# Graph kernel of four layers: the beginning of layer 3 in another order (alternate chunks per tile, reads ahead of casts, parts spread over nine steps), and the last layernorm in three tiles

## The chip, the cores and the metric

The kernel runs on one core of one Trainium2 chip. The metric is the device time of one execution in microseconds (us); less is better. Five engines work side by side, each through its own queue in order: TensorE (PE, matmuls; its weight loads are shown as PEld), VectorE (DVE), ScalarE (ACT), GpSimd (POOL) and SyncE (SP, which here only issues transfers).

## The reference

3327 nodes with 64 features, and a dense weighted adjacency `adj`. Four layers, each followed by a residual and a layernorm:

```python
x = _layernorm(x + _L0_gnn_ref(t, x, adj))       # 1 - 0.1 x - 0.01 sum(x * (adj @ x)), constant per node
x = _layernorm(x + _L1_gnn_ref(x, adj, att_W, att_b))   # hyperbolic attention over all pairs
x = _layernorm(x + _L2_gnn_ref(x, adj, W))
x = _layernorm(x + _L3_gnn_ref(x, adj, weight, bias))
# layer 2, two hops
for k in range(2):
    agg = adj @ x
    x = jnp.tanh(jnp.concatenate([agg, x], axis=1) @ W[k])
# layer 3: each node takes its last 100 neighbours, the last with weight 1, each before with half of the next
support = x @ weight
mask = (adj != 0); rank = jnp.cumsum(mask, axis=1); deg = rank[:, -1:]
k = jnp.minimum(deg, 100.0); pos = rank - (deg - k)
w = mask * jnp.where(pos > 0, 0.5 ** (k - pos), 0.0)
out = w @ support + bias
```

## The kernel before

Nodes are padded to 26 blocks of 128 (`NB`), in two halves of 13; `adj` is held transposed in HBM, and a block is 128 rows of it by 3328 columns, 1.7 MB. The last four blocks stay in SBUF for the whole run (`kept`), two more for layer 2; the others are streamed by SP's queue into a few slots, and a slot's next transfer waits until PE has read the slot. The instructions of PE, ACT and DVE stand in the order in which the code writes them (`manual_schedule`); each engine takes its queue in order, and an instruction that must wait holds all behind it on its engine. [...]

**End of layer 1** (`near_end`). A serial chain of small operations on 128x26 numbers goes back and forth between DVE and ACT (one tanh, two square roots). PE has nothing to do but a few idle matmuls (`awake`). At the end DVE writes x2 in five groups (L1441), the last operand of each in a PSUM tile `pm`.

**Layer 2** (`layers`, first part). x2 is transposed (`turned`, L339), multiplied with the upper half of W (`top`, L349, into `lj`), and then for each block eight matmuls (`add`, L395) add to four chunks of 416 columns in both halves, in the four banks of two PSUM tiles `cnt`: chunks 0 and 1 in the first tile, 2 and 3 in the second. `bottom` (L386) adds x times the lower half of W. Two hops; `chunk_end` adds the last two or three kept blocks for one chunk and takes the tanh on ACT (L471). In the second hop the order of blocks is: six that are still in SBUF from the first hop, then the kept ones with five streamed blocks behind each. Between, `pw_3` (L436) multiplies layer 3's weight with the centring matrix, and ACT copies it back (L437).

**Layer 3.** For every step q (half h, block jb from the last to the first, 52 steps in all) DVE makes a mask (L331, three steps ahead), PE counts with two triangular matrices (`count` and `advance`, L491) into `cnt[0]` and `cnt[1]`, whose bits read as int16 are the bf16 powers of two (`read`: ACT L506 or DVE L504), and PE multiplies these weights `w` with the node values (`products`, L689, and every three steps a group of twelve for the lowest part, L704). Reading `cnt[c]` and advancing it exclude each other. In the loop, ACT reads chunk 0 and DVE chunk 1. The node values are split in three bf16 parts (`first_part`, `rest_of`, `other_parts`: ACT, DVE, then ACT and POOL).

**The beginning of layer 3** is written out by hand and overlaps the end of hop 2. The blocks come in four parts A, B, C, E. For each: `finish` (PE, L558, tile `both`, two buffers), `squares` (ACT), `sums` and `roots` (DVE, nine short operations), `factor` and `x3_of` or `hid_out`, then the split. The first steps' reads and advances stand between. With the loop's first steps (q from `LEAD`, which is 3) stand the splits of C and E, three operations in one step each:

```python
with_step = {
    LEAD: lambda: (first_part(C), rest_of(C), other_parts(C)),
    LEAD + 1: lambda: (first_part(E), rest_of(E), other_parts(E)),
    LEAD + 2: lambda: x3_later(C),
    LEAD + 3: lambda: x3_later(E),
}
```

**Half ends.** After a half's 26 steps, `sums_out` moves the sums to SBUF (ACT and DVE, a chunk each), `sum_of_parts` turns them back to rows by node in 13 matmuls of two passes (L729, one PSUM tile `pr_o`), and a layernorm follows: `half_out` for the first half, a piece with each step of the second, and `last_out` for the second half, in three groups of nodes (6, 4, 3).

Of the kernel before, what the change touches and what calls it, by code (L numbers as in the profile page):

```python
# [10 lines left out]
F32 = mybir.dt.float32  # L11
# [62 lines left out]
def kernel(  # L74
# [220 lines left out]
    def layer_3_constants():  # L295
# [2 lines left out]

        nc.gpsimd.tensor_scalar(w3_dg, w3_dg, float(2**27), None, ALU.mult)


    @with_exitstack
    def layers(ctx, x2, x3, kept, ready, ahead_ctx, strm):
# [41 lines left out]
        def node_products(ps, hT, w, g, n, name):  # L345
# [11 lines left out]
        x2T = x3.rearrange("p n d -> p (n d)")  # L357
        hT = x2T
        l3c = ctx.enter_context(
            tc.tile_pool(name="l3c", bufs=1, space=PSUM, reuse_waits="tile")  # L360
        )

        cnt = [l3c.tile([P, 2, 512], F32, name=f"cnt_{c}")[:, :, :CW] for c in range(2)]
        acc = [cnt[c // 2][:, c % 2, :] for c in range(CPH)]
        pinned = ctx.enter_context(ExitStack())
        pinned.enter_context(
            tc.manual_schedule(engines={mybir.EngineType.DVE, mybir.EngineType.Activation})
# [1 line left out]
        with tc.tile_pool(name="l2p", bufs=2, space=PSUM, reuse_waits="tile") as l2p:  # L369
            for k in range(2):  # L370
# [39 lines left out]
                others = [jb for jb in range(NB) if jb not in kept and jb not in ready]  # L410
                share = -(-len(others) // len(stay))
                order = list(ready)
                for i, jb in enumerate(stay):
                    order += [jb] + others[i * share : (i + 1) * share]
                blocks = {**ready, **kept}

                if k == 0:
                    turned(0)
                    turned(1)
                    top(0, nc.scalar.copy)  # L420
                    turned(2)
# [12 lines left out]

                    pw = l2p.tile([P, 4 * P], F32, tag="pt", name="pw_3")[:, :P]
                    nc.tensor.matmul(pw, center, w3_dg, start=True, stop=True)  # L436
                    nc.scalar.copy(w3_dg, pw)  # L437

                    warm_t = small.tile([P, 1], F32, tag="warm", name="warm_t")
                    nc.scalar.activation(warm_t, ones, AF.Tanh)  # L440
                    order = order[2:]
                else:
                    top(0)
                    bottom(0)
                    bottom(1)
# [153 lines left out]
        def x3_of(i):  # L599
            scaled(i, both[i][0], x3)  # L600
# [19 lines left out]
        with tc.tile_pool(name="l3t", bufs=2, space=PSUM, reuse_waits="tile") as l3t:  # L620
            chunk_end(3)
            with_x2(3)
            chunk_end(2)
            with_x2(2)
            finish(l3t, A)
            squares(A)
            chunk_end(1)
            sums(A)
            roots(slots(A))
            factor(A)  # L630
            with_x2(1)
            finish(l3t, B)
            squares(B)
            x3_of(A)
            sums(B)
            first_part(A)
            count(1, tri, 0, True)
            read(1, 0, False)
            rest_of(A)
            chunk_end(0)  # L640
            roots(slots(B))
            with_x2(0)
            other_parts(A)
            finish(l3t, C)
            count(0, tri, 0, True)
            advance(1, 0)
            squares(C)
            read(0, 0, False)
            factor(B)
            x3_of(B)  # L650
            first_part(B)
            sums(C)
            finish(l3t, E)
            hid_out(C)
            advance(0, 0)
            rest_of(B)
            read(1, 1, True)
            squares(E)
            hid_out(E)
            advance(1, 1)  # L660
            read(0, 1, False)
            other_parts(B)
            sums(E)
            advance(0, 1)
            roots(slice(0, 2 * sum(parts[C])))
            read(1, 2, False)
            advance(1, 2)
            read(0, 2, False)
            advance(0, 2)
            factor(C)  # L670
            factor(E)

        l3a = ctx.enter_context(
            tc.tile_pool(name="l3a", bufs=2, space=PSUM, reuse_waits="tile")
# [45 lines left out]
            nc.vector.tensor_scalar(to[1], acc[h, 1], b3_sb, None, ALU.add)  # L720
            return accT

        def sum_of_parts(h, accT):

            pr = acc_tile(f"pr_o_{h}").rearrange("p e k -> p (e k)")[:, : NBH * D]
            pr = pr.rearrange("p (n d) -> p n d", d=D)
            xh, hh, sh = (by_half(t)[:, :, h] for t in (x3, hid, sq))
            for b in range(NBH):
                nc.tensor.matmul(  # L729
                    pr[:, b, :], accT[:, b * P : (b + 1) * P], center2, start=True, stop=True  # L730
                )
            return pr, xh, hh, sh
# [10 lines left out]
        def last_out(h, accT):  # L743

            pr, xh, hh, sh = sum_of_parts(h, accT)
            v = small.tile([P, NBH], F32, tag="v_out", name=f"v_out_{h}")
            parts = (slice(0, 6), slice(6, 10), slice(10, NBH))

            def added(s):
                nc.vector.tensor_tensor(hh[:, s], pr[:, s], xh[:, s], ALU.add)  # L750
                nc.scalar.activation(sh[:, s], hh[:, s], AF.Square)

            def summed(s):
                nc.vector.tensor_reduce(v[:, s], sh[:, s], axis=AX.X, op=ALU.add)

            added(parts[0])
            added(parts[1])
            summed(parts[0])
            added(parts[2])
            summed(parts[1])  # L760
            summed(parts[2])
            r = rsqrt_of(v, NBH)

            rows = N - h * HALF - (NBH - 1) * P
            for s, queue in zip(parts, (nc.sync, nc.scalar, nc.sync)):
                nc.vector.tensor_tensor(
                    hh[:, s], hh[:, s], spread(r[:, s], s.stop - s.start), ALU.mult
                )
                if store(queue, h, hh, s):
                    nc.scalar.dma_start(out[N - rows :], hh[:rows, NBH - 1])  # L770

        def half_out(h, accT):

            pr, xh, hh, sh = sum_of_parts(h, accT)
            v = small.tile([P, NBH], F32, tag="v_out", name=f"v_out_{h}")
            parts = (slice(0, 8), slice(8, NBH))
            yield
# [9 lines left out]
            for s in parts:  # L787
# [3 lines left out]
                store(nc.sync, h, hh, s)  # L791
                yield

        first_out = None
        with_step = {
            LEAD: lambda: (first_part(C), rest_of(C), other_parts(C)),
            LEAD + 1: lambda: (first_part(E), rest_of(E), other_parts(E)),
            LEAD + 2: lambda: x3_later(C),
            LEAD + 3: lambda: x3_later(E),
        }  # L800
        for q in range(LEAD, len(steps) + LEAD + 1):
            read(0, q, False)
            read(1, q, True)
            if q == NB + LEAD:
                accT = sums_out(0)
            masks(q + AHEAD)
            with_step.pop(q, lambda: None)()
            p = q - LEAD if q < NB + LEAD else q - LEAD - 1
            for c in range(2):
                if q < len(steps):  # L810
                    advance(c, q)
                if q != NB + LEAD:
                    products(p, c)
            if q == NB + LEAD:
                first_out = half_out(0, accT)
            if first_out is not None:
                next(first_out, None)
        last_out(1, sums_out(1))

# [14 lines left out]
    with tc.tile_pool(name="l1", bufs=1) as l1:  # L834
# [426 lines left out]
        def near_end(mT, xm, sq_e, t_e, x2):  # L1261
# [3 lines left out]
            with tc.tile_pool(name="l1e", bufs=1) as l1e, tc.tile_pool(  # L1265
# [395 lines left out]
        with norms.Else():  # L1661
            with ExitStack() as arm:
                x1 = xc
                with tc.tile_pool(name="g1m", bufs=1) as g1m:
                    m = g1m.tile([P, NB, D + 1], F32, name="m")
                    any_norm(m, x1)
                    layer_3_constants()
                    blocks = blocks_ahead(arm)
                    any_end(m, x1, x2)
                layers(x2, xc, *blocks)  # L1670
# [31 lines left out]
```

## Time and profile before

| | us |
|---|---|
| median of 3 runs | 576.31 (576.22 to 577.29) |
| the profiled execution | 575.76 |
| its span, first to last instruction | 573.9 |
| layer 1, attention (until the last pq) | about 222 |
| end of layer 1, to the first transposed x2 | 222 to 244 |
| layer 2, hop 1 and hop 2 | 244 to 330, 330 to 414 |
| layer 3, both halves | 404 to 559 |
| last layernorm and store | 559 to 574 |

The page gives busy time by engine; the waits say who waited for whom on an engine; the stretches give busy time of each engine within a window; the timeline shows single instructions with their start. Times are from one profiled execution. The mean granted PE clock is 0.985 of full speed.

### The profile page before, as it was taken

Reading aid. Unit: us, or ns where it says so; the run is one execution under the profiler, and the core shown is the slowest. Engines: PE = TensorE matmul, PEld = TensorE weight load, DVE = VectorE, ACT = ScalarE, POOL = GpSimd, SP = SyncE. Lnnn points to the kernel's source line nnn. Section 1 sums busy time; section 2 is a strip of 40 time slices with the busy share of each in tenths; the row PEclk is TensorE's granted clock in tenths of the full one; section 3 lists DMA queues with packets and bytes.
Section 4 is the critical chain, followed back from the end, with each engine's and each line's share of the span. In section 5 each row is a group of like instructions: output and inputs, shape, how many; then the busy total and the mean of one; then the engine's idle time right before and its main releaser. Section 6 shows DMA issues by size and latency. Waiting matters only on the chain.

```text
span 573.9 us, 7452 instructions
## 1 busy us (share of the span) xinstructions
PE 529.7 (92%) x2827; PEld 223.3 (39%) x2827; DVE 364.6 (64%) x528; ACT 276.7 (48%) x329; POOL 216.9 (38%) x134
## 2 busy tenths in 40 slices
PE   8899989999999999689999999998989999999992
PEld 5522222222222224254444354433444555555542
DVE  6899999999999998920000010400388777797724
ACT  4899999998999997321000100000263333343321
POOL 3799999999999998100000000000020000000000
PEclk9899999999999999989999999999999999999996
DMA  8976765750767653999999029998608996699701
GB/s 290 358 270 211 225 216 206 233 184 1 230 208 221 233 181 120 399 428 404 421 429 408 10 99 422 370 423 351 239 13 296 322 334 230 208 282 366 246 2 35
DMA packets 34037, 145.27 MB, mean 253 GB/s; under 512 B 10285, under 2 KB 11975, under 8 KB 28871
## 3 DMA queue, kind: packets, MB, share of 16 engines
q1 hardware_dynamic: 31655, 144.11, 69.0%
q10 hardware_dynamic: 2336, 0.59, 0.5%
q8 instruction: 24, 0.39, 0.3%
q14 instruction: 22, 0.18, 0.1%
HBM read 143.23 MB, written 0.87 MB: 251 GB/s over the span
## 4 chain that ended last, share of the span: by engine, by line
PE 63%; DVE 19%; ACT 8%; DMA 4%; issue 4%; POOL 0%; DVEq 0%; POOLq 0%
PE cnt L395 22%; PE pq L1028 12%; DVE v L1049 12%; PE cnt L491 11%; PE acc L689 6%; DMA at_l<-in_adjT 4%; ACT sg L1004 3%; PE acc L704 3%; ACT pq L1041 2%; DVE a L1040 2%; PE pn_l L349 1%; PE both L558 1%; PE pr_o L729 1%; PE cnt L386 1%; PE idle L864 1%
## 5 line engine op out<-in xcount | busy, mean ns | idle before, releaser
L1015 POOL TENSOR_TENSOR u<-sg,at 128x832 f32<-128x832 f32 x88 | 169.9, 1958 | 3.1 <-ACT sg L1004 2.7
L1028 PE MATMUL pq<-riT,ljT 64*128 64x416 f32 x416 | 100.2, 560 | 15.2 <-DVE v L1049 6.3
L1040 DVE SCALAR_TENSOR_TENSOR a<-pq,dl,u 128x832 f32<-128x832 f32 x104 | 112.0, 1077 | 3.0 <-PE pq L1028 2.9
L1041 ACT ACTIVATE pq<-pq,al,gas 128x832 f32<-128x832 f32 x104 | 104.9, 1010 | 15.2 <-DVE a L1040 14.2
L1049 DVE SCALAR_TENSOR_TENSOR v<-pq,a 128x832 f32<-128x832 f32 x104 | 105.6, 1016 | 1.1 <-ACT pq L1041 0.7
L1061 PE MATMUL acc<-v,xv 128*64 128x416 f32 x416 | 95.4, 537 | 0.1
L395 PE MATMUL cnt<-at_l,lj 128*64 128x416 f32 x480 | 86.5, 513 | 2.1 <-DMA at_l<-in_adjT 2.1
L1004 ACT ACTIVATE sg<-lb,rb 128x1664 f32<-128x1664 f32 (+1 forms) x53 | 87.3, 1647 | 0.1
L506 ACT ACTIVATE w<-cnt 128x832 int16<-128x832 f32 x54 | 46.5, 864 | 72.3 <-PE cnt L491 72.3
L471 ACT ACTIVATE hT<-cnt 128x416 f32<-128x416 f32 x8 | 4.1, 517 | 146.0 <-PE cnt L395 146.0
L618 POOL TENSOR_TENSOR s<-sq,s 128x384 bf16<-128x384 f32 (+1 forms) x4 | 4.1, 1025 | 185.9 <-ACT s L617 185.9
L504 DVE TENSOR_SCALAR w<-cnt 128x832 int16<-128x832 f32 x50 | 51.2, 1023 | 25.4 <-PE cnt L491 25.0
L1028 PEld LDWEIGHTS pq<-riT,ljT 64*128 64x128 f32 x416 | 31.5, 184 | 88.3 <-DVE v L1049 83.0
L383 DVE COPY lj<-pn_l 128x384 f32<-128x384 f32 (+2 forms) x8 | 4.3, 541 | 89.5 <-PE pn_l L349 89.5
L491 PE MATMUL cnt<-mask,rest 128*128 128x416 bf16 x200 | 51.6, 339 | 4.1 <-ACT w L506 4.0
L395 PEld LDWEIGHTS cnt<-at_l,lj 128*64 128x64 f32 x480 | 34.0, 137 | 51.4 <-issue 46.4
L491 PE MATMUL cnt<-mask,tri 128*128 128x416 bf16 x208 | 53.5, 339 | 0.1
L689 PE MATMUL acc<-w,s 128*128 128x416 bf16 x208 | 52.6, 339 | 0.0
L1061 PEld LDWEIGHTS acc<-v,xv 128*64 128x64 f32 x416 | 20.6, 134 | 61.0 <-issue 57.8
L331 DVE TENSOR_SCALAR mask<-ah 128x1664 bf16<-128x1664 f32 x42 | 43.5, 1035 | 0.0
L395 PE MATMUL cnt<-kept,lj 128*64 128x416 f32 x192 | 36.1, 515 | 1.9 <-ACT hT L471 1.9
L1015 POOL TENSOR_TENSOR u<-sg,kept 128x832 f32<-128x832 f32 x16 | 31.1, 1972 | 3.7 <-ACT sg L1004 3.6
(280 smaller groups left out, 393.6 us busy)
## 6 DMA issues: line engine op xcount, KB each, us to landing
at_l<-in_adjT SPq DMA_DIRECT2D x26, 1664.0 KB, 11.8
at<-in_adjT SPq DMA_DIRECT2D x44, 832.0 KB, 5.0
ah<-in_adjT SPq DMA_DIRECT2D x42, 832.0 KB, 6.3
bt_l<-in_adjT SPq DMA_DIRECT2D x8, 1664.0 KB, 9.9
kept<-in_adjT SPq DMA_DIRECT2D x6, 1664.0 KB, 9.1
lb<-lf_rows SPq DMA_DIRECT2D x2, 384.0 KB, 5.1
ljT<-ljT SPq DMA_DIRECT2D x4, 128.0 KB, 6.8
x<-in_x ACTq DMA_DIRECT2D x1, 416.0 KB, 5.4
```

The lines of the kernel that those rows point to most:

```text
L395: nc.tensor.matmul(acc[c][h * D : (h + 1) * D, :], hw[:, slot(jb), :], blocks[jb][:, o : o + CW], start=c not in begun, stop=last, skip_gr ...
L491: nc.tensor.matmul(cnt[c][:, e, :], mat, mask[q][:, of], start=start, stop=(mat is tri), skip_group_check=True,)
L504: nc.vector.tensor_scalar(w.bitcast(I16), cnt[c], 0.0, None, ALU.max)
L506: nc.scalar.activation(w.bitcast(I16), cnt[c], AF.Relu)
L689: nc.tensor.matmul(acc[h, c][:, e, :], s12[:, slot(jb)].rearrange("p t d -> p (t d)"), ws[q, c][:, e, :], start=first, stop=last,)
L1004: nc.scalar.activation(sg[:, :, of], lbs[:, :, of], AF.Sigmoid, bias=rb[:, sl : sl + 1])
L1015: nc.gpsimd.tensor_tensor(u, sg[:, :, of], at[:, :, of], ALU.mult)
L1028: nc.tensor.matmul(pq[:, h, :], ljT[h != jb // NBH][rows, of], riT[rows, ch * CW : (ch + 1) * CW], start=True, stop=True,)
L1040: stt(a_s[t], pqs[t], dl[:, one], us.pop(t), op0=ALU.add, op1=ALU.mult)
L1041: nc.scalar.activation(pqs[t], pqs[t], AF.Square, bias=al[:, one], scale=gas[:, one])
L1049: stt(w, pqs.pop(t), CUBIC_REST, a_s.pop(t), op0=ALU.add, op1=ALU.mult)
L1061: nc.tensor.matmul(accs[cp, ci][h * D : (h + 1) * D, :], xv[:, slot(jb), :], w[:, h, :], start=(jb == order[0]), stop=(jb == order[-1]),)
```

## The change

Six things are done. (1) The matmul and copy that centre layer 3's weight move out of layer 2 to the end of layer 1, behind an idle matmul there. (2) The two `cnt` tiles lie at the right side of PSUM, and the four chunks of layer 2 alternate between them: 0 and 2 in the second tile, 1 and 3 in the first. (3) In hop 2 five streamed blocks come before the first kept one, then three behind each. (4) At the beginning of layer 3, the counts start with the other tile, reads of `cnt` stand ahead of casts and copies, all six first reads are on ACT, and the splits are spread over nine steps, one operation a step, placed ahead of that step's mask; in the loop the products of a step stand ahead of the advance. (5) At the turn between halves, the matmuls by node come in two parts, one behind each advance. (6) In the last layernorm the three groups of nodes go into three PSUM tiles, the two `cnt` tiles among them.

```diff
+    def centred_weights(ps):
+        pw = ps.tile([P, P], F32, name="pw_3")
+        nc.tensor.matmul(pw, center, w3_dg, start=True, stop=True)
+        nc.scalar.copy(w3_dg, pw)
...
-            tc.tile_pool(name="l3c", bufs=1, space=PSUM, reuse_waits="tile")
+            tc.tile_pool(name="l3c", bufs=1, space=PSUM, side="right", reuse_waits="tile")
...
-        acc = [cnt[c // 2][:, c % 2, :] for c in range(CPH)]
+        acc = [cnt[1 - c % 2][:, c // 2, :] for c in range(CPH)]
...
+                if k:
+                    order, others, share = order + others[:5], others[5:], 3
...
-                    pw = l2p.tile([P, 4 * P], F32, tag="pt", name="pw_3")[:, :P]
-                    nc.tensor.matmul(pw, center, w3_dg, start=True, stop=True)
-                    nc.scalar.copy(w3_dg, pw)
...
             first_part(A)
-            count(1, tri, 0, True)
-            read(1, 0, False)
+            count(0, tri, 0, True)
+            read(0, 0, False)
...
             finish(l3t, C)
-            count(0, tri, 0, True)
-            advance(1, 0)
+            count(1, tri, 0, True)
             squares(C)
-            read(0, 0, False)
             factor(B)
             x3_of(B)
+            read(1, 0, False)
+            sums(C)
             first_part(B)
-            sums(C)
             finish(l3t, E)
+            rest_of(B)
             hid_out(C)
+            squares(E)
             advance(0, 0)
-            rest_of(B)
-            read(1, 1, True)
-            squares(E)
-            hid_out(E)
+            sums(E)
+            read(0, 1, False)
+            advance(1, 0)
+            roots(slice(0, 2 * sum(parts[C])))
+            read(1, 1, False)
+            advance(0, 1)
+            read(0, 2, False)
             advance(1, 1)
-            read(0, 1, False)
-            other_parts(B)
-            sums(E)
-            advance(0, 1)
-            roots(slice(0, 2 * sum(parts[C])))
             read(1, 2, False)
-            advance(1, 2)
-            read(0, 2, False)
-            advance(0, 2)
             factor(C)
             factor(E)
+            hid_out(E)
+            advance(0, 2)
...
+        with_step = [
+            lambda: other_parts(B), lambda: first_part(C), lambda: rest_of(C),
+            lambda: other_parts(C), lambda: first_part(E), lambda: rest_of(E),
+            lambda: other_parts(E), lambda: x3_later(C), lambda: x3_later(E),
+        ]
+        products(0, 0)
+        advance(1, 2)
+        products(0, 1)
         for q in range(LEAD, len(steps) + LEAD + 1):
+            turn = q == NB + LEAD
             read(0, q, False)
+            if turn:
+                first_out = half_out(0, sums_out(0))
             read(1, q, True)
-            if q == NB + LEAD:
-                accT = sums_out(0)
+            if with_step:
+                with_step.pop(0)()
             masks(q + AHEAD)
-            with_step.pop(q, lambda: None)()
             p = q - LEAD if q < NB + LEAD else q - LEAD - 1
             for c in range(2):
+                if p and not turn:
+                    products(p, c)
                 if q < len(steps):
                     advance(c, q)
-                if q != NB + LEAD:
-                    products(p, c)
-            if q == NB + LEAD:
-                first_out = half_out(0, accT)
-            if first_out is not None:
+                if turn:
+                    next(first_out)
+            if first_out is not None and not turn:
                 next(first_out, None)
...
+            by_node(accT, pr, slice(0, 6))
+            yield
+            by_node(accT, pr[:, 6:], slice(6, NBH))
+            yield
...
+            prs = [places(t) for t in (*banks, acc_tile(f"pr_o_{h}"))]
+            for pr, s in zip(prs, parts):
+                by_node(accT, pr, s)
...
                 vec(u2, u2, gq, add)
                 awake(u2)
+                centred_weights(l1t)
```

More of the change, by code (lines that the diff above doesn't have):

```diff
@@ L359, in layers @@
         l3c = ctx.enter_context(
-            tc.tile_pool(name="l3c", bufs=1, space=PSUM, reuse_waits="tile")
+            tc.tile_pool(name="l3c", bufs=1, space=PSUM, side="right", reuse_waits="tile")
         )
-        cnt = [l3c.tile([P, 2, 512], F32, name=f"cnt_{c}")[:, :, :CW] for c in range(2)]
-        acc = [cnt[c // 2][:, c % 2, :] for c in range(CPH)]
+        banks = [l3c.tile([P, 2, 512], F32, name=f"cnt_{c}") for c in range(2)]
+        cnt = [b[:, :, :CW] for b in banks]
+        acc = [cnt[1 - c % 2][:, c // 2, :] for c in range(CPH)]
         pinned = ctx.enter_context(ExitStack())
@@ L721, in sums_out, with by_node, places, in_half @@
             return accT
[L723 to L728, printed above, removed]
+        def by_node(accT, pr, s):
+            for b in range(s.start, s.stop):
                 nc.tensor.matmul(
-                    pr[:, b, :], accT[:, b * P : (b + 1) * P], center2, start=True, stop=True
-                )
-            return pr, xh, hh, sh
+                    pr[:, b - s.start, :], accT[:, b * P : (b + 1) * P], center2,
+                    start=True, stop=True,
+                )
+        def places(tile):
+            return tile.rearrange("p e k -> p (e k)")[:, : NBH * D].rearrange(
+                "p (n d) -> p n d", d=D
+            )
+        def in_half(h):
+            return (by_half(t)[:, :, h] for t in (x3, hid, sq))
         def store(queue, h, hh, s):
@@ L741, in store, with half_out @@
             return last < s.stop
-        def last_out(h, accT):
-            pr, xh, hh, sh = sum_of_parts(h, accT)
+        def half_out(h, accT):
+            pr = places(acc_tile(f"pr_o_{h}"))
+            xh, hh, sh = in_half(h)
             v = small.tile([P, NBH], F32, tag="v_out", name=f"v_out_{h}")
[L747 to L775, printed above, removed]
+            by_node(accT, pr, slice(0, 6))
+            yield
+            by_node(accT, pr[:, 6:], slice(6, NBH))
+            yield
             parts = (slice(0, 8), slice(8, NBH))
-            yield
             for s in parts:
@@ L792, in half_out, with last_out, added, summed @@
                 yield
-        first_out = None
[L795 to L800, printed above, removed]
+        def last_out(h, accT):
+            xh, hh, sh = in_half(h)
+            v = small.tile([P, NBH], F32, tag="v_out", name=f"v_out_{h}")
+            parts = (slice(0, 6), slice(6, 10), slice(10, NBH))
+            prs = [places(t) for t in (*banks, acc_tile(f"pr_o_{h}"))]
+            for pr, s in zip(prs, parts):
+                by_node(accT, pr, s)
+            def added(k):
+                s = parts[k]
+                nc.vector.tensor_tensor(hh[:, s], prs[k][:, : s.stop - s.start], xh[:, s], ALU.add)
+                nc.scalar.activation(sh[:, s], hh[:, s], AF.Square)
+            def summed(k):
+                s = parts[k]
+                nc.vector.tensor_reduce(v[:, s], sh[:, s], axis=AX.X, op=ALU.add)
+            added(0)
+            added(1)
+            summed(0)
+            added(2)
+            summed(1)
+            summed(2)
+            r = rsqrt_of(v, NBH)
+            rows = N - h * HALF - (NBH - 1) * P
+            for s, queue in zip(parts, (nc.sync, nc.scalar, nc.sync)):
+                nc.vector.tensor_tensor(
+                    hh[:, s], hh[:, s], spread(r[:, s], s.stop - s.start), ALU.mult
+                )
+                if store(queue, h, hh, s):
+                    nc.scalar.dma_start(out[N - rows :], hh[:rows, NBH - 1])
@@ L1667 @@
                     layer_3_constants()
+                    with tc.tile_pool(name="g3", bufs=1, space=PSUM) as g3:
+                        centred_weights(g3)
                     blocks = blocks_ahead(arm)
```

## The prediction

> **What bounds the kernel now.** I read the page first: one engine fills the span, and its clock is granted in full.
>
> ```profile
> PE 529.7 (92%) x2827; PEld 223.3 (39%) x2827; DVE 364.6 (64%) x528; ACT 276.7 (48%) x329; POOL 216.9 (38%) x134
> ```
>
> TensorE (PE) is busy in 529.7 of 573.9 us. The diff removes no matmul, so it can only win what PE doesn't do: waits, cold clock and the ends where PE is done. The second view is the list of waits of PE from 240 us on (who waits for whom: us, times, longest):
>
> ```profile
> PE cnt L491 <- ACT w L506: 4.0, 6, 1.0
> PE pt_x L339 <- DVE x L1441: 2.7, 2, 2.1
> PE cnt L395 <- DMA at_l<-in_adjT: 2.1, 3, 1.0
> PE cnt L395 <- ACT hT L471: 1.9, 3, 0.6
> ```
>
> These four rows, 10.7 us, lie at the places that the diff edits. Third, the stretches (length, then PE, PEld, DVE, ACT, POOL busy, granted clock, DMA share, GB/s):
>
> ```profile
> 246.20:248.00 1.80, 1.76 (x9) 1.76 (x10) 0.00 (x0) 0.48 (x1) 0.00 (x0) 0.54 0.94 399
> ...
> 403.87:418.22 14.35, 13.73 (x70) 6.50 (x67) 7.54 (x28) 4.61 (x9) 0.28 (x1) 1.00 0.61 238
> 418.22:437.00 18.78, 15.29 (x86) 8.18 (x85) 16.94 (x29) 11.07 (x18) 3.82 (x4) 1.00 0.36 110
> 437.00:488.00 51.00, 50.94 (x318) 27.01 (x317) 39.74 (x42) 18.13 (x21) 0.00 (x0) 1.00 0.84 295
> ```
>
> Layer 3's steady loop (437 to 488) is PE without a gap: nothing to win. Its beginning (404 to 437) loses 4.1 us, and 418 to 437 has DVE 90% busy. At 246 us, after a wait of 2.11 us, PE runs at 0.54 of its clock. Last, the timeline of the end:
>
> ```profile
> 559.73 3.12 PE L729 MATMUL pr_o<-center,accT 128*128 128x64 f32 x26
> 562.89 0.89 DVE L750 TENSOR_TENSOR hid<-pr_o,xc 128x384 f32<-128x384 f32 x2 [2.14 <-PE pr_o L729]
> ```
>
> DVE adds the first six nodes only when all 26 passes into the one tile are done.
>
> [...] Here it fell to 0.54 to 0.56 from 246.2 to 250.0, after PE had been busy for 0.13 of 2.2 us; gaps of 1.2 to 1.5 us between the idle matmuls before (234 to 242) left it at 1.00. That POOL and DVE disturb each other I take from the trace alone: the masks at 430 and 433 us took 1.30 and 1.53 us beside POOL's subtraction, 1.02 elsewhere.
>
> **The change part by part.**
>
> 1. *Weights centred earlier (pw_3).* Layer 2 loses a matmul of 0.31 us (261.07 to 261.38). It now stands behind the first idle matmul of layer 1's end, which ends at 235.08, and its copy stands on ACT ahead of the tanh. In the trace of before that copy starts 0.42 us after its matmul and takes 0.27, so the tanh starts at 235.77, not 234.96: +0.81 us on a serial chain of ACT and DVE. The next idle matmul behind it comes 0.3 us later, and nobody waits for that one. Net +0.5.
>
> 2. *Counts on the right side of PSUM.* By the build, x2's second transposed tile (pt_x) shares a bank with the last norm product before; afterwards it doesn't. It waited until 246.18 for the last L1441; its own rows are ready at 244.40 (second L1441). Then ACT's bx, busy until 245.3, is late next: its copies end at 245.70 and 246.18. So the first pn group goes at 245.75, not 246.87: at least 1.12 us. PE now idles 0.75 us at most, less than the gaps that left the clock full; at full clock the two pn groups take about 0.7 each and the transposes 0.4 (rows of 252 to 255), so the first add (L395) starts at 247.55, not 250.02: 2.47 us. Items 1 and 2 together: 2.0 warm, 0.6 cold. A transfer limits it: the last block of the first hop is issued at 303.55, lands 15.0 later, at 318.55, and is used at 320.1; DMA is saturated (426 GB/s), so much more than 1.45 us can't come through. I take **1.5** (0.4 to 2.2).
>
> 3. *Alternate chunks (acc over the two tiles).* At the first hop's end two waits of 0.62 us for tanh (rows of 325.07 and 328.70) go: the next chunk's adds of 1.4 us lie between. **1.24**. The third such wait is in item 5.
>
> 4. *Blocks of hop 2.* Five streamed blocks come ahead of the kept ones. Each block is 2.8 us of PE and 4.0 of DMA (1.70 MB at 426 GB/s). Before, DMA has a hole from 365 to 375 us, about 0.85 MB or 2.0 us: the seventh block's slot came free only at 364.9. Now its reader comes one kept block earlier (362.1), and each later slot comes free before DMA needs it. The last block then lands 2.0 us sooner, 398.95; without waits PE wants it at 401.02 less 2.07, the same moment. **2.0** (1.0 to 2.1).
>
> 5. *Layer 3's beginning.* I added PE's work from chunk 3 to the end of the first L704 group: 4 chunks x 2.25, four `both` groups 1.49 + 1.39 + 1.40 + 1.80, two counts x 0.36, 12 advances x 0.70, 6 products x 0.35, 1.18: 27.5 us. Before it took 403.87 to 436.62, 32.75 us. I then set the new order out on ACT, DVE and PE with the durations of before (read 0.87 on ACT, 1.02 on DVE; cast 0.5; root step 0.2; 0.06 per handover). The same method gives 5.5 us of waits for the old order, against 5.2 measured. What remains in the new one: the last `both` group comes right behind one count, and its bank waits for x3_of(B), whose DVE chain (8.1 us unbroken) starts only 0.62 earlier: 0.8 to 1.2. Four reads on ACT (3.5 us), hid_out(E) 0.6, which now waits for factor(E) on DVE, and read(0,3) behind it hold the advances by 0.3, 0.2, 0.2 and 0.4. The waits of 0.95, 0.87 and 0.85 behind casts go, since a cast now stands behind its step's read and its DVE partner is a step earlier. Waits 2.2, so 29.7 us: **3.0** (2.2 to 3.5). DVE in the later steps: read 1.02, mask 1.02 and every few steps 0.55, against 2.5 of PE on average; three masks of reserve hide it. If POOL's three remaining subtractions each hold a mask by 0.5, this is 0.5 less.
>
> 6. *The turn (two parts of by_node between the advances).* Same 26 passes. The one wait there (0.5, for the read behind the squares) stays, as the squares keep their step. **0**, +0.5 to -0.5[...].
>
> 7. *Last layernorm in three tiles.* Twelve passes (1.4 us) release the first add at 561.2, not 562.89. DVE: 0.55, 0.35, sum 0.55; the last tile is done at 562.85 and its add comes at 563.05; its square (0.36) and the two sums end at 564.25, against 565.64. **1.4** (1.0 to 1.7). The banks of the counts are free by then (last read 553).
>
> No DMA is added, and SP's queue keeps its order; the loads for the masks (ah), which take the streamed blocks' place and were first issued at 404.08, move with the blocks and are next needed three steps later. The sum is 1.5 + 1.24 + 2.0 + 3.0 + 0 + 1.4 = 9.1 us. The profiled execution took 575.76 us (span 573.9 and 1.86 around it), so 566.7; the median of the runs, 576.31, is 0.55 above it, so 567.2.
>
> **The rivals.** *New waits take the old ones' place* (0.28): the clock stays cold (0.6 instead of 1.5), the landing of hop 2's blocks stays late (1.0), `both` E, hid_out(E) behind DVE and POOL eat more of the beginning (2.0), the turn costs 0.5, the end gives 1.1: 5.4 us, 570.9. For it: DVE is at 90% there, and the new order leaves it all but one read. Against it: the method fits the old order to 0.3 us. *Slower* (0.06): in the loop, products now precede each advance. Between the advances of one chunk lie 0.35 + 0.70 + 0.35 = 1.40 us as before, and a DVE read with its handovers takes 1.14; read and mask fill 2.04 of a bare step of 2.11. If reads come late by x in each of some 47 steps, that is 47x; from x = 0.19 the 9.1 us are gone, and at x = 0.25 it is 579. Against it: the cycle of three operations is the same, only begun elsewhere, and PE shows no gap in it. *The edits don't reach the path* (0.04): 575 to 577.
>
> **How the numbers follow.** Forecast 0.62, at 567.2. Low ends of the items together are 11.2 us (565.1), high ends 5.3 (571.0); I give 565.0 to 571.2, which takes in the first rival. A change of 0.2% (1.15 us) is about what a measurement here can tell: faster 0.90 (forecast and first rival), same 0.04, slower 0.06.
>
> **What would show it.** Right: the L491 waits on ACT fall from 4.0 to some 1.5 us, those of L395 on hT and on DMA to under 0.4, PE's clock stays at 1.00 around 247, the chunk-3-to-burst stretch takes 29.7 us, and the end from the first pr_o pass to the last sum 4.5 us instead of 5.9. Wrong in a step: a tanh not late by 0.8; a PE wait of over 1.5 us for DVE before the last `both`. Wrong altogether: gaps of PE in the steady steps.

## The result, and the profile after

The changed kernel takes 567.44 us (median, 566.39 to 569.11; 4 runs) against 576.26 us before: ratio 0.985, 95% interval 0.982 to 0.988, 8.8 us less. The profiled execution took 566.58 us, span 564.9 (before 575.76, span 573.9). PE's row on the page:

```profile
PE 527.5 (93%) x2827; PEld 221.9 (39%) x2827; DVE 362.7 (64%) x527; ACT 277.3 (49%) x330; POOL 216.7 (38%) x134
```

Of the 9.0 us between the spans, 2.2 are busy time of PE, most of it the half clock at 246 us (1.7, see the experiments); the rest are waits and ends. The list of waits of PE from 225 us on (us in total, times, longest), without those of the idle matmuls (4.4 us before, 4.8 now), in the new line numbers (L403 is `add`, L498 `count`, L345 the transposes, L355 the node products, L565 `finish`, L694 the products, L1467 the last step of x2, L766 the add of the first half's layernorm):

```profile
PE pt_x L345 <- DVE x L1467: 0.9, 2, 0.6
PE pn_l L355 <- ACT xc L349: 0.8, 1, 0.8
PE both L565 <- DVE xc L598: 0.6, 1, 0.6
PE cnt L498 <- ACT w L513: 0.6, 3, 0.2
PE cnt L403 <- DMA at_l<-in_adjT: 0.6, 1, 0.6
PE acc L694 <- DVE hid L766: 0.5, 1, 0.5
PE cnt L498 <- DVE w L511: 0.4, 2, 0.2
```

The four rows of before, 10.7 us, have become 4.4 us in seven rows. The waits for a tanh (hT) are gone; the counts wait 0.6 for ACT instead of 4.0; new are the waits for ACT's copy before the first node products, for DVE before the last `both` and for `hid` at the turn. The stretches that answer to those shown of before (length, then PE, PEld, DVE, ACT, POOL busy, granted clock, DMA share, GB/s); the second and third are the beginning of layer 3, now from 398.56:

```profile
246.20:248.00 1.80, 1.45 (x13) 1.46 (x14) 0.78 (x3) 1.15 (x4) 0.00 (x0) 1.00 0.96 404
398.56:412.91 14.35, 14.04 (x72) 6.69 (x68) 8.37 (x29) 5.24 (x11) 1.12 (x1) 1.00 0.62 238
412.90:431.00 18.10, 16.98 (x95) 9.35 (x96) 13.79 (x25) 11.72 (x18) 1.84 (x3) 1.00 0.36 117
```

PE's clock at 246 us is 1.00. In the third stretch PE is busy 94% of the time (before 81%), and DVE 76% (before 90%), since operations on DVE moved into the loop. Last, the timeline of the end:

```profile
551.84 2.44 PE L731 MATMUL cnt<-center,accT 128*128 128x64 f32 x20
553.50 0.56 DVE L792 TENSOR_TENSOR hid<-cnt,xc 128x384 f32<-128x384 f32 x1 [0.65 <-PE cnt L731]
...
555.39 0.87 DVE L797 TENSOR_REDUCE v_out<-sq 128x4 f32<-128x256 f32 x2
```

DVE's first add comes 1.66 us after the first pass, not 3.16. The whole difference, from the starts of the same work in the two timelines (before less after):

| up to | before | after | gain in this stretch |
|---|---|---|---|
| the third block's adds in hop 1 | 261.38 | 259.55 | 1.83 (items 1 and 2) |
| first node product of hop 2 | 330.25 | 326.74 | 1.68 (item 3) |
| chunk 3 at hop 2's end | 403.87 | 398.56 | 1.80 (item 4) |
| first burst of low parts and twelve advances done | 436.62 | 428.40 | 2.91 (item 5) |
| first pass of the last layernorm | 559.73 | 551.84 | -0.33 (loop and turn, item 6) |
| last sum | 565.64 | 556.26 | 1.49 (item 7) |
| end of the span | 573.9 | 564.9 | -0.4 (the stores; up to their issue nothing is lost) |

0.14 of the first row was there before the change begins: layer 1's end began that much earlier in this execution.

### The profile page after: what moved, and what is told of

It is laid out like the page before. It is cut to its first block, busy times and chain, and to the rows that moved or that the text cites. A ratio compares the mean times of both kernels' runs of the same rounds, so it can differ in the third digit from the quotient of the medians.

```text
span 564.9 us, 7457 instructions
## 1 busy us (share of the span) xinstructions
PE 527.5 (93%) x2827; PEld 221.9 (39%) x2827; DVE 362.7 (64%) x527; ACT 277.3 (49%) x330; POOL 216.7 (38%) x134
## 4 chain that ended last, share of the span: by engine, by line
PE 63%; DVE 20%; ACT 8%; issue 5%; DMA 2%; DVEq 0%; POOL 0%; POOLq 0%
PE cnt L403 23%; PE pq L1053 12%; DVE v L1074 12%; PE cnt L498 11%; PE acc L694 6%; ACT sg L1029 4%; PE acc L709 3%; ACT pq L1066 2%; DVE a L1065 2%; DMA at_l<-in_adjT 2%; PE pn_l L355 1%; DVE w L511 1%; PE cnt L394 1%; DVE mask L337 1%; PE idle L889 1%
## 5 line engine op out<-in xcount | busy, mean ns | idle before, releaser
L403 PE MATMUL cnt<-at_l,lj 128*64 128x416 f32 x480 | 86.3, 513 | 0.6 <-DMA at_l<-in_adjT 0.6
L403 PEld LDWEIGHTS cnt<-at_l,lj 128*64 128x64 f32 x480 | 34.0, 137 | 50.0 <-issue 47.7
L498 PE MATMUL cnt<-mask,tri 128*128 128x416 bf16 x208 | 53.5, 339 | 0.1
L694 PE MATMUL acc<-w,s 128*128 128x416 bf16 x208 | 52.6, 339 | 0.5 <-DVE hid L766 0.5
L498 PE MATMUL cnt<-mask,rest 128*128 128x416 bf16 x200 | 51.6, 340 | 1.2 <-ACT w L513 0.6
L403 PE MATMUL cnt<-kept,lj 128*64 128x416 f32 x192 | 35.5, 513 | 0.0
```

The costliest lines, as they stand in the source:

```text
L403: nc.tensor.matmul(acc[c][h * D : (h + 1) * D, :], hw[:, slot(jb), :], blocks[jb][:, o : o + CW], start=c not in begun, stop=last, skip_gr ...
L498: nc.tensor.matmul(cnt[c][:, e, :], mat, mask[q][:, of], start=start, stop=(mat is tri), skip_group_check=True,)
L694: nc.tensor.matmul(acc[h, c][:, e, :], s12[:, slot(jb)].rearrange("p t d -> p (t d)"), ws[q, c][:, e, :], start=first, stop=last,)
```

## The experiments

My theory: the gains stand at the places of the seven items, nearly all of each reaches the end, and none depends on another. The rival: a few waits hang together, and what one edit wins is lost at the next transfer or wait. Medians of one kernel differ by up to a microsecond from one measurement to the next (the kernel before: 576.1 to 577.0), so the stretch in the trace decides. The median beside it is a weaker sign of whether the gain reached the end: with an item undone it lies 1.2 to 2.0 us above the kernel after each time, but each interval (the ratio to the kernel before, in brackets) overlaps with that of the kernel after, 0.9816 to 0.9881. Item 6 was not undone by itself.

**Two kernels on the clock, from the kernel before.** Idle matmuls are put in PE's wait of 2.1 us:

```diff
                     turned(0)
+                    for _ in range(6):        # before_fill3: range(3)
+                        nc.tensor.matmul(acc[0], w2_dg[:, 1, :], list(kept.values())[0][:, :CW], ...)
                     turned(1)
```

> The kernel before, with six idle matmuls (128 x 128 into 416 columns, 0.35 us each, into a count bank that is not yet in use) between x2's first and second group of transposes, that is in the 2.1 us in which PE waits for the last L1441 of layer 1. My theory (PE's clock fell to half because PE had nothing to do there): the wait's end stays where it was, near 246.2 us, the clock is 1.00 from 246 to 250, and the first add comes at about 248.7 instead of 250.0: 1.35 us less, 574.9. Rival (the clock follows something else, such as the DMA load or the idle stretches of layer 1's end before it): still 0.54 to 0.56 behind the matmuls, no gain, or up to 0.2 us more where the last idle matmul outlasts the wait.

Measured: 576.75 us against 576.25, ratio 1.0005 (0.9994 to 1.0016). The clock stayed at 1.00, but each matmul took two passes, 4.36 us for the six, and the second group of transposes began at 248.47 instead of 246.24. From there to the first add it was 2.09 us instead of 3.78: the half clock costs 1.7 us, not 1.35. So the kernel was repeated with three:

> The kernel before, with three idle matmuls in the 2.1 us wait instead of six. The variant with six kept the clock full, but each matmul took two passes of 0.36 us, so that the six (4.36 us) outlasted the wait by 2.2 us and gave the gain back. Theory: three end within 0.2 us of the wait's end; from there to the first add PE needs 2.1 us as with six, not 3.8: the first add comes 1.4 to 1.7 us earlier than in the kernel before, 574.7. Rival (blocks' landings take the gain back in the first hop, as my step had it): the first add is early, the second hop's first node product isn't, 576.2.

Measured: 574.41 us against 577.02 measured beside it, ratio 0.9965 (0.9951 to 0.998). The timeline of the kernel before, then of this one:

```profile
246.24 0.83 PE L339 MATMUL pt_x<-ident,x 128*128 128x128 f32 x3 [2.11 <-DVE x L1441]
...
250.02 3.02 PE L395 MATMUL cnt<-at_l,lj 128*64 128x416 f32 x16
```

```profile
246.17 0.55 PE L339 MATMUL pt_x<-ident,x 128*128 128x128 f32 x3
246.56 0.83 PE L349 MATMUL pn_l<-w_dg,xc 128*128 128x128 f32 x6
...
248.32 3.01 PE L395 MATMUL cnt<-at_l,lj 128*64 128x416 f32 x16
```

The wait ends where it did, and the first add comes 1.70 us earlier, at full clock; at the first node product of hop 2 (328.69) 1.56 of it is left. So the rival, that the blocks take the gain back, falls. But the limit that the forecast set on item 2 showed itself: the last block of hop 1 was issued at 301.8, not 303.5, took 16.6 us instead of 15.0 and landed at 318.4, when PE was there. The list of PE's waits doesn't have it, because the weight load (PEld) took the wait:

```profile
318.48 0.20 PEld L395 LDWEIGHTS cnt<-at_l,lj 128*64 128x64 f32 x4 [0.65 <-DMA at_l<-in_adjT]
```

The adds of the two blocks around it take 5.74 us from start to start, and 5.58 in the kernel before; that is the difference between 1.70 and 1.56.

**Counts on the left again, from the kernel after** (`side="right"` taken out).

> The kernel after, with the counts on the left side of PSUM as before. Theory: x2's second transposed tile shares a bank with layer 1's last product again, waits about 2.1 us, the clock falls to 0.54 to 0.56, and the first add comes 2.4 us later than in the kernel after (near 250.8); all later work moves with it, +2.4 us, 569.8. Rival (the blocks' landings limit the first hop, as the step of the forecast had it): PE catches up before 320 us, since the blocks land when they landed, and only 1.5 us or less is left at the end of the first hop.

Measured: 568.73 us (ratio to before 0.9861, 0.9839 to 0.9883). PE waited 1.50 before the transposes and 0.94 before the first node product, and the clock was 0.51 from 248 to 251.4. From the idle matmul at `e_u` to the first add it took 16.34 us, against 14.35 in the kernel after: 2.0 us, not 2.4. At hop 2's first node product it was still 2.0 (94.68 against 92.68 us from the same start). So the tiles' place costs this much and the hop doesn't win it back, as the theory has it, with a size 0.4 too big; but the waits fall on the first transposes and the first node product, and not on the second group of transposes.

**Chunks in pairs in hop 1, alternate in hop 2.**

```diff
+                acc = [
+                    cnt[1 - c % 2][:, c // 2, :] if k else cnt[c // 2][:, c % 2, :]
+                    for c in range(CPH)
+                ]
```

> The kernel after, with the first hop's chunks in pairs in the count tiles (0 and 1, then 2 and 3) as before; the second hop keeps alternate chunks. Theory: the two waits of 0.62 us for a tanh come back at the first hop's end, and each costs about 0.84[...]: 1.68 us by the first node product of hop 2. At the end of hop 2 0.6 of it may be won back, where PE waits 0.59 us for a block: +1.1 to +1.7, 568.5 to 569.1. Rival (the wait costs what the list of waits says): +1.24 us by the same place, +0.6 at the end.

Measured: 569.45 us (0.9877, 0.9853 to 0.99). The end of hop 1 and the start of hop 2:

```profile
323.70 1.57 PE L407 MATMUL cnt<-kept,lj 128*64 128x416 f32 x8
325.88 3.02 PE L407 MATMUL cnt<-kept,lj 128*64 128x416 f32 x16 [0.61 <-ACT hT L482]
329.51 1.62 PE L407 MATMUL cnt<-kept,lj 128*64 128x416 f32 x8 [0.61 <-ACT hT L482]
331.06 1.16 PE L355 MATMUL pn_l<-w_dg,hT 128*128 128x128 f32 x8
```

7.36 us for the 32 adds, 5.69 in the kernel after: 1.67 for two waits that are listed with 1.22. At the block that came late in hop 2 nothing was won back (0.59 again): when PE comes later, so do the slots and the transfers (hop 2's first issue of `at_l` at 346.29 us instead of 341.97). This execution showed something else too. It began layer 2 with the same three short waits as the kernel after, but:

```profile
246.20:248.00 1.80, 0.95 (x6) 0.72 (x7) 1.80 (x6) 1.71 (x7) 0.00 (x0) 0.97 0.99 422
248.00:251.30 3.30, 3.30 (x16) 2.91 (x17) 0.39 (x2) 0.96 (x2) 0.00 (x0) 0.50 1.04 438
```

Half clock for 3.3 us, 1.4 lost up to the first add. Of the six profiled kernels whose order is that of the kernel after up to here and whose counts stand on the right, without idle matmuls, five kept the full clock (1.00 from 244 to 251 us). In all six PE's three gaps here were the same, 0.57, 0.32 and 0.75 us (0.76 once); in the kernel before, gaps of 1.20 to 1.47 us between 234 and 242 us left the clock at 1.00, and one of 2.11 us had 0.54 behind it. So the length of the gaps does not tell the one profile from the five; what does, no run shows.

**Hop 2's blocks in the old order** (the line that sets `order`, `others` and `share` for k = 1 taken out).

> The kernel after, with the second hop's blocks in the old order (kept and streamed ones in turn). Theory: the three waits for blocks come back, 2.1 us in all instead of 0.6[...]: from the second hop's first node product to chunk 3, 73.6 us instead of 71.8, +1.8 us, 569.2. Rival (PE now reaches the hop 3.5 us earlier and outruns the transfers, whose pace is set elsewhere): waits of over 3.5 us, +3 or more.

Measured: 568.84 us (0.9877, 0.9858 to 0.9895), 1.4 above the kernel after. The waits for blocks:

```profile
PE cnt L403 <- DMA at_l<-in_adjT: 1.9, 3, 1.0
```

From hop 2's first node product (326.47) to chunk 3 (399.96) it took 73.5 us, 1.7 more. The stretch where the transfers pause, first in this kernel, then in the kernel after (last column GB/s):

```profile
360.00:365.00 5.00, 5.00 (x32) 2.12 (x30) 3.24 (x4) 0.00 (x0) 0.00 (x0) 1.00 0.90 335
365.00:370.00 5.00, 5.00 (x32) 2.04 (x30) 0.00 (x0) 0.00 (x0) 0.00 (x0) 1.00 0.99 389
```

```profile
360.00:365.00 5.00, 5.00 (x32) 2.07 (x30) 0.71 (x1) 0.00 (x0) 0.00 (x0) 1.00 1.01 426
365.00:370.00 5.00, 5.00 (x30) 2.01 (x28) 0.00 (x0) 0.00 (x0) 0.00 (x0) 1.00 1.01 426
```

91 GB/s less for 5 us and 37 for another 5 are 0.64 MB, or 1.5 us at 426 GB/s: the hole of item 4. The waits grew no further although PE reached the hop 3.8 us earlier than in the kernel before; the rival falls.

**The beginning of layer 3 and the loop as before** (the block of reads, advances, casts, and the loop are those of the minus lines of the diff, with the two count tiles renamed).

> The kernel after, with the beginning of layer 3 and the loop's order as before (the two count tiles change names, so that the tile whose chunks end first is counted first; the turn keeps its two parts). Theory: the waits behind casts and behind one DVE read come back, and from chunk 3 to the end of the same work (the first burst of low parts and the advance behind it) PE needs 31.9 to 32.8 us instead of 29.8: +2.1 to +2.9 us, 569.5 to 570.3. Rival (most of the stretch's gain came from the chunks' alternation, which stays here): under +1.

Measured: 568.66 us (0.9875, 0.9858 to 0.9892). PE's waits for reads on ACT:

```profile
PE cnt L498 <- ACT w L513: 4.2, 6, 1.5
```

Chunk 3 starts at 398.40, the burst at 429.14, its end at 430.32: 31.9 us for the work that takes 29.84 in the kernel after. So 2.08 us of item 5 are the order, and the other 0.83 fit the third tanh wait (0.84 for each of the first two), which the alternate chunks take away.

**Only the parts piled up again**: the new beginning, but the nine operations in four steps of the loop.

```diff
-            lambda: other_parts(B), lambda: first_part(C), lambda: rest_of(C),
-            lambda: other_parts(C), lambda: first_part(E), lambda: rest_of(E),
-            lambda: other_parts(E), lambda: x3_later(C), lambda: x3_later(E),
+            lambda: (other_parts(B), first_part(C), rest_of(C), other_parts(C)),
+            lambda: (first_part(E), rest_of(E), other_parts(E)),
+            lambda: x3_later(C), lambda: x3_later(E),
```

> The kernel after, with the parts for the products made in two steps of the loop as before (four operations in the first, three in the second, the two scalings in the third and fourth), instead of one operation in each of nine steps; the beginning of layer 3 stays in the new order. Theory: the second cast of a group stands on ACT ahead of the next read and waits for a subtraction on DVE that stands behind a read and a mask; the two longest waits of the old order (1.5 and 0.85 us) come back, and the stretch from chunk 3 to the same work takes 31.3 to 32.0 us instead of 29.8: 569.0 to 569.7. Rival (the new order ahead of the loop gives the gain, as it does the reads first): +0.5 at most.

Measured: 569.03 us (0.9877, 0.9858 to 0.9897); the stretch takes 31.34 us (398.33 to 429.67). ACT and the PE wait behind it, from the timeline:

```profile
422.66 0.51 ACT L624 CAST s<-sq 128x384 bf16<-128x384 f32 x1 [1.03 <-DVE sq L620]
423.08 0.86 ACT L513 ACTIVATE w<-cnt 128x832 int16<-128x832 f32 x1
```

```profile
423.99 0.51 PE L498 MATMUL cnt<-mask,rest 128*128 128x416 bf16 x2 [1.19 <-ACT w L513]
426.63 0.51 PE L498 MATMUL cnt<-mask,rest 128*128 128x416 bf16 x2 [0.38 <-ACT w L513]
```

ACT stands idle for 1.03 us in front of the second cast, whose subtraction is late on DVE, and the read that PE needs stands behind that cast. So some 1.5 of the 2.08 us come from one operation for each step, and 0.6 from the order ahead of the loop and in it. The split is rough, since the first step here has four operations and had three in the kernel before. The rival had it the other way round.

**The last layernorm in one tile** (26 passes into one `pr_o`, the adds unchanged).

> The kernel after, with the last layernorm's 13 nodes in one tile of PSUM again. Theory: the first add waits for all 26 passes, 5.9 us from the first pass to the last sum instead of 4.4, +1.5 us at the end, 568.9. Rival (the end is set by the last transfer's completion, or the three tiles' adds are held by something else): under +0.5 us.

Measured: 568.81 us (0.9873, 0.9849 to 0.9897). First pass at 551.80, first add at 554.95, and the root 1.45 us later than in the kernel after (557.74 against 556.29); the span is 1.4 longer. The gain of item 7 reaches the end in this execution.

**Three small additions to the kernel after.** First the centred weights behind the tanh:

```diff
-                centred_weights(l1t)                       # after awake(u2)
...
                 nc.scalar.activation(warm_e[:, :1], ones, AF.Sqrt)
+                centred_weights(l1t)
```

> The kernel after, with layer 3's centred weights one step later: their matmul behind the second idle matmul of layer 1's end, their copy on ACT behind the tanh and the load of the root's table. Theory: the tanh starts 0.2 us after its argument, as in the kernel before, and DVE's chain from there to x2 ends 0.8 us earlier: -0.8 us, 566.6, provided the clock behind it is the same. Rival (another engine's work, not this chain, sets the end of layer 1): the tanh is earlier, the first group of x2's transposes isn't.

Measured: 566.69 us (0.9841, 0.9823 to 0.986). From the idle matmul at `e_u` to the first transposes it took 9.41 us, as before the change (9.42), against 10.35: the copy ahead of the tanh costs 0.93. But in the profiled execution the clock fell to 0.50 at 246 us, and the first add came at 248.57, no earlier than in the kernel after. PE's gaps there were the same (0.57, 0.32, 0.75). That the lower median comes from the earlier tanh is not shown.

Then idle matmuls in the three gaps (`fill` writes to places of the same PSUM tile that nobody reads), alone and with the weights:

```diff
+        def fill(to, times):
+            for _ in range(times):
+                nc.tensor.matmul(to, ident, center, start=True, stop=True)
...
-                    turned(0)
-                    turned(1)
-                    top(0, nc.scalar.copy)
+                    turned(0, 2)
+                    turned(1, 1)
+                    top(0, nc.scalar.copy, 3)
```

> The kernel after, with six short idle matmuls (two passes of 128 columns each) in PE's gaps of 0.57, 0.32 and 0.75 us around layer 2's first two groups of transposes (two, one and three of them), written to places of the same tiles that nobody reads. Theory: the gaps leave the kernel after on the edge, its clock at 246 to 251 us is full in some executions and half in others (1.00 in its profile, 0.50 in that of the variant with chunks in pairs, with the same three gaps), which is 1.4 us each time. With the fillers it is full in all: the profile shows 1.00, the first add comes no later than 0.2 us after its place, and the median falls by some 0.7 us to 566.7, with the runs closer together than 566.4 to 569.1. Rival (the half clock has another cause, or is rare): no change, 567.4.

Measured: 567.44 us (0.9851, 0.9833 to 0.987; 566.88 to 568.62), the clock at 1.00, the first add at 248.34. The median is that of the kernel after. It settles nothing on the clock, since a wait in hop 2 grew by 1.7 us (below).

> The kernel after, with both small changes: the centred weights behind the tanh, and the six short idle matmuls in PE's gaps at layer 2's start. Theory: x2's first transposes stand at 243.3 us as with the centred weights alone, and the clock, which fell to 0.50 there, stays at 1.00; the first add comes at 247.3 instead of 248.4 (after) or 248.6 (weights alone). Median 565.9 at most, below both kernels. Rival (the next thing late takes it: the first hop's blocks): the first add is early, but PE waits for a block before 320 us, and 566.7 stays.

Measured: 566.11 us (564.78 to 567.21; 0.9812, 0.9794 to 0.9831), the lowest median of all; against the kernel after (0.9816 to 0.9881) the intervals still overlap. The first add comes at 247.51, at full clock, 0.9 earlier. In both kernels with six idle matmuls a wait had grown, and not before 320 us but in hop 2:

```profile
PE cnt L409 <- DMA at_l<-in_adjT: 2.3, 1, 2.3
```

The blocks' bytes had all but stopped 2 us before its end, and a transfer of instructions (16 KB) stood in it. The last kernel has four idle matmuls (one, one, two):

> The kernel after, with the centred weights behind the tanh and four idle matmuls (one, one and two) instead of six. With six, PE waited 2.3 us before the last streamed block of hop 2 instead of 0.6, although the blocks' bytes had stopped arriving 2 us before its end; the only other transfer there was one of PE-side instructions (16 KB at 394 us; at 396 in the kernel after). Theory (the longer program moves an instruction fetch into that wait): with eight PE passes fewer the wait is 0.5 to 0.7 again, the first add stays at 247.5, the clock at 1.00, and the time falls by some 1.6 us against six, 564.6. Rival (PE comes too early for the block and waits for its landing): 2.3 us again, 566.1.

Its wait is back at 0.59, and its span of 563.7 us is the shortest of the profiled executions:

```profile
394.94 3.01 PE L409 MATMUL cnt<-at_l,lj 128*64 128x416 f32 x16 [0.59 <-DMA at_l<-in_adjT]
```

It reached this block at 394.35 us, the kernel with six at 394.10; an arrival 0.25 us earlier doesn't explain a wait that is 1.7 us longer, so the rival falls. That it was the fetch of instructions fits, but was only argued. PE also came too early for the last block of hop 1 here: the weight load waited 0.81 us for it (to 317.35), and the two blocks' adds took 5.89 us. And the gain does not show in the times: 566.96 us median (565.41 to 567.81; 0.9842, 0.982 to 0.9864). Whether four or six are better stays open.

## Why the prediction was right

The time (567.2 forecast, 567.44 measured) and nearly every step came out. The sum was 9.1 us; the spans differ by 9.0. That it fits so closely is in part luck: items 1 to 3 brought 0.8 more than forecast, and item 4, the loop with the turn, and the stores, which the sum left out, lost 0.9.

- *Items 1 and 2*, 1.5 forecast, 1.83 measured. The tanh was late by the 0.8 of the forecast (`e_uy` at 236.02, not 235.22; with the 0.14 of the earlier start 0.94). First before, then after:

```profile
234.96 0.23 ACT L1366 ACTIVATE e_tanh<-e_th 128x26 f32<-128x26 f32 x1 [5.11 <-DVE e_th L1363]
235.22 0.19 DVE L1277 TENSOR_TENSOR e_uy<-e_tanh,e_ux 128x26 f32<-128x26 f32 x1 [0.29 <-ACT e_tanh L1366]
```

```profile
235.60 0.27 ACT L305 COPY both_m<-pw 128x128 f32<-128x128 f32 x1 [5.89 <-issue]
235.76 0.23 ACT L1392 ACTIVATE e_tanh<-e_th 128x26 f32<-128x26 f32 x1
236.01 1.28 ACT L1394 ACT_TABLE_LOAD   x1
236.02 0.19 DVE L1302 TENSOR_TENSOR e_uy<-e_tanh,e_ux 128x26 f32<-128x26 f32 x1 [1.23 <-ACT e_tanh L1392]
```

  With the clock kept, this is 1.69 without the 0.14, against 2.0 in the forecast's warm case and 1.5 after its limit. The limit by the last block's landing is real, but was set at a wrong place: the forecast took issue and landing as fixed. The issue waits for a slot which PE frees. In the kernel after it came at 301.71 instead of 303.55, and the block landed at 317.4 instead of 318.5, before PE wanted it (318.3). It took 15.7 us instead of 15.0, and in the kernel before with three idle matmuls 16.6, where it landed only 0.1 us earlier and PE lost 0.15. So an issue that comes 1.8 us earlier moves the landing by 0.1 to 1.1; what sets it within this range no run shows.
- *Item 3*, 1.24 forecast, 1.68 measured: the term was mis-sized. Each wait of 0.62 costs 0.84: eight adds end 1.57 us after the first one's start, but without a wait the next ones begin after 1.4, so a wait loses this overlap too. What these waits kept apart were not the same columns: by the code each chunk has its own half of the tile (512 columns), and the tanh of chunk 0 reads one half while the adds of chunk 1 write the other. The program orders them by tile (`reuse_waits="tile"`), and with the chunks in different tiles neither wait is left.
- *Item 4*, 2.0 forecast, 1.80 measured (1.7 when undone). One of three waits stayed (0.59, where the forecast allowed under 0.4): the transfers' hole closed as forecast, but PE's need and the landing meet only to within 0.6 us.
- *Item 5*, 3.0 forecast, 2.91 measured, to 29.84 us (29.7). The waits stand where the setting-out had them: 0.63 before the last `both` (0.8 to 1.2 forecast), then 0.25, 0.20 and 0.18 for reads on ACT (four of 0.2 to 0.4 forecast). One of 0.17 for a read on DVE was not in it: that read stood behind a mask which took 1.71 us beside POOL's subtraction (0.91 us); the next two masks, with none beside them, took 1.01 and 1.02. That DVE has room in the loop's first steps was right, and matters most, by the piled kernel.
- *Item 6*, 0 forecast, 0.33 lost, within its range. The wait at the turn is as long as before but has another cause: products for the next half need a PSUM tile that DVE's `hid` add hasn't yet left. So the waits on ACT fell to 0.6 and not to 1.5. From the burst to the last layernorm it takes 123.44 us, 123.33 with the old loop and the new turn (whose one wait is 0.9 there, not 0.5), and 123.11 before: the loop with the products first costs a few tenths at most, and the rival on the other side, late reads in every step, didn't occur.
- *Item 7*, 1.4 forecast, 1.49 measured.

## What to carry to other kernels

Where a profile shows many short waits at places that don't touch, add up PE's work in a stretch, set the new order out by hand on each engine, and take each removed wait at its listed length plus the lost overlap (0.2 us here). Where a transfer's landing looks like a limit, look at what released its issue and at how busy the transfers are: here the slot followed the engine that became faster by 1.8 us, and the landing by 0.1 to 1.1; in both traces, before and after, the transfers moved 425 GB/s from 300 to 312 us. Look at the waits of the weight loads too; the list of PE's waits can hide a late block (here 0.65 and 0.81 us). And spread operations that hop between engines one to a step: two of them in one step put a wait for the other engine in front of work that the bottleneck needs.

## What the runs showed of the hardware

- Behind gaps of 0.57, 0.32 and 0.75 us PE's clock was at 0.50 for 3.3 us in one of six profiles of the same order up to there, and at 0.50 from 246 to 249 us in one of a kernel with the same three gaps; in the other five of the six it stayed at 1.00.
- Three idle matmuls (2.26 us) in a wait of 2.11 us left the clock behind it at 1.00 instead of 0.54 and won 1.7 us up to the first add, though the wait ended no sooner (246.17 against 246.24); six (4.36 us) outlasted it and won nothing.
- In two profiles with six short matmuls more at 244 us a wait at 394 us was 2.3 us instead of 0.6, in one with four it was 0.6; the cause was only argued. One profile of such a variant is not enough to judge it.
- A block's transfer issued 1.8 us earlier took 15.7 us to land in the kernel after, and 16.6 in the kernel before with three idle matmuls, instead of 15.0, while the transfers moved 425 GB/s (300 to 312 us, in the traces of before and after).
